# Turning the experts' gate-up product between partition groups on VectorE, in place of a trip through DRAM

## The chip, the cores and the metric

The kernel runs on one core of a Trainium2 chip. A core has TensorE (PE, matrix products; PEld is its weight load), VectorE (DVE), ScalarE (ACT), GpSimd (POOL) and SyncE (SP), each with an instruction stream of its own, and 16 DMA engines that move data between DRAM and the on-chip memories (SBUF, 128 partitions, and PSUM, where products land). Engines wait for one another through semaphores. The metric is the device time of one execution in microseconds. Three runs before the change took 3898.57, 3900.75 and 3912.13 us; the median is 3900.75.

## The reference

The reference is a decoder layer in float32 on x of shape (32, 128, 512): differential self-attention, cross-attention against a context of the same shape, and a feed-forward part with experts. The last one is what matters here, on 4096 tokens of 512 features:

```python
scores = jax.nn.sigmoid(x @ gate_w)            # 32 experts; masked by groups
_, selected_experts = jax.lax.top_k(masked_scores, K)      # K = 6
xs = x_exp[sort_idx]                           # tokens sorted by expert
g = jax.lax.ragged_dot(xs, w_gate, group_sizes)            # 512 -> 352
u = jax.lax.ragged_dot(xs, w_up, group_sizes)
d = jax.lax.ragged_dot(jax.nn.silu(g) * u, w_down, group_sizes)   # 352 -> 512
expert_out = jnp.sum(out * weights[..., None], axis=1)
shared = jax.nn.silu(x @ sw_gate) * (x @ sw_up) @ sw_down
return (expert_out + shared).reshape(B, S, H)
```

So each token goes through six experts, each expert is a gate product, an up product, their combination and a down product, and the six results are added with weights.

## The kernel before

The stages follow one another: self-attention, cross-attention with the routing, three of eight groups of the shared feed-forward part, the experts, and the other five shared groups. In the trace the experts take from about 2024 to 3617 us.

**Tiles.** Routing puts each expert's tokens into tiles of 128 slots, each tile with tokens of one expert only; 208 tiles are run. `SETS = 4` sets of weight tiles (`wg`, `wu`, `wd`) stand in SBUF, and tile i uses set i % 4. The tiles are so ordered that tiles i and i+4 mostly belong to one expert. A weight DMA has a condition (`cond=new`): it moves data only where the expert of the set changes.

**The steps of a tile i.**
- `tokens(i)` (L1422): four indirect DMAs issued by POOL gather the 128 tokens' rows from DRAM into `e_xr` (three buffers). Each row of 512 features is gathered in four runs of 128 (`Q = 4`), so that partition 32 q + k gets run q of four tokens. 
- `turn_in(i)` (L1434): one DVE turn of all 32x32 blocks makes `e_xT`, features on partitions, tokens along the row.
- `gate_up(i)` (L1447): eight gate and up products on PE (sixteen matmul instructions in the trace, since a float32 product takes two) give a PSUM tile with tokens on partitions; ACT makes Silu of the gate half (`e_act`, L1451) and DVE multiplies by the up half into `gu_s` (called `e_gu`, L1452).
- The down product needs `e_gu` with its 352 columns on partitions. DVE turns only within 32x32 blocks, that is, within a group of 32 partitions. To bring a column range of 96 (`RUN`) to each of the four groups, ACT's queue writes `e_gu` to DRAM (`e_gu_d`, L1454), and `part_out(i)` (L1463) reads it back as `e_gr`, with run q of four tokens on each partition of group q.
- `turn_out(i)` (L1473): two DVE turns, one for the first three groups (three chunks of columns) and one for the last group (two chunks, as 352 = 3 x 96 + 64), make `e_guT` (two buffers).
- `down(i)` (L1483): three chunks of products; ACT scales by the routing weight (`e_y`, L1487); POOL scatters with addition into `sum_d` in DRAM (L1488).
- `weights_in` (L1396) and `weights_out` (L1408, L1411) issue the weight DMAs on SP's queue.

Because a partition of `e_gr` holds four tokens in turn, as `e_xr` does, the order of the tokens in a turned tile is a permutation. `arrange` (L1338) lays out the gather's table so that the reading through DRAM is contiguous: it interleaves the slot numbers.

**The order.** PE, DVE, ACT and POOL run in the order in which `run` (L1508) writes the calls; SP's work is placed by the scheduler with the constraint `issue_after`. In one step of the loop the calls are: `gate_up(i)`, `turn_in(i + 2)`, `turn_out(i - 1)`, `weights_in(i + 4)`, `down(i - 2)`, `weights_out(i + 2)`, `part_out(i)`, `tokens(i + 5)`. So PE does gate and up of tile i and then down of tile i-2. ACT does Silu(i), issues the write of e_gu, scales tile i-2, and issues the read of e_gr, all in order.

Of the kernel before, what the change touches and what calls it, by code (L numbers as in the profile page):

```python
# [10 lines left out]
F32 = mybir.dt.float32  # L11
I32 = mybir.dt.int32
AF = mybir.ActivationFunctionType
ALU = mybir.AluOpType
AX = mybir.AxisListType
PSUM = bass.MemoryType.PSUM
DRAM = bass.MemoryType.DRAM

P = 128
# [9 lines left out]
M = 352  # L29
# [6 lines left out]
class Common:  # L36


    def __init__(self, tc, const, psum):
        nc = self.nc = tc.nc  # L40
        self.tc = tc
        self.psum = psum
        self.ident = const.tile([P, P], F32, name="ident")
        make_identity(nc, self.ident)
        self.mhalf = const.tile([P, 16], F32, name="mhalf")
        nc.vector.memset(self.mhalf, -0.5)
# [53 lines left out]
class Later:  # L100
# [8 lines left out]
    def run(self, step, phase):  # L109

        while self.calls and self.calls[0][0] <= (step, phase):
            _, call, args = self.calls.pop(0)
            call(*args)


def self_attention(cm, x, x1_d, Wq, Wk, Wv, Wo, lq1, lk1, lq2, lk2, heads, heads_in, beside):
# [19 lines left out]
    with ExitStack() as ctx:  # L136
# [342 lines left out]
        for n in range(len(steps) + 5):  # L479
# [29 lines left out]
            if k % 2 == 0:  # L509
                if 3 in at:  # L510
                    with behind():
                        norms(at[3][0])
                measure(b)
                if 4 in at:
                    load_again(at[4][0])
            else:
                normalize(b)
                turn_in(b)
                load(b + G)
                if 4 in at:  # L520
                    with behind():
                        scale_out(at[4][0])
                    turn_out(at[4][0])
# [4 lines left out]
class CrossAttention:  # L528
# [224 lines left out]
    def turn_out(self, b):  # L753
        o = self.out.pop(b)
        self.out[b] = self.p2.tile([P, E], F32, name="xoT")
        self.nc.vector.transpose(self.out[b], o.rearrange("p k s c -> p (k s c)"))
# [90 lines left out]
    def advance(self, count, end=None):  # L847


        steps, behind = self.steps, self.S + self.LAG  # L850
        for _ in range(count):
            n = self.at
            if n >= (self.SMALL if end is None else end):
                return
            self.at += 1
            first, sooner, middle, after, later = self.PHASES
            run = self.todo.run
            run(n, sooner)
            if 0 <= n - behind < len(steps):
                self.exponentials(*steps[n - behind])  # L860
            run(n, middle)
            if 0 <= n < len(steps):
                self.maxima(*steps[n])
            run(n, later)
# [400 lines left out]
class Experts:  # L1265
# [14 lines left out]
    def __init__(  # L1280
        self, cm, ctx, table_ds, h3_d, sum_d, w_gate, w_up, w_down, eid, fresh, rows, n_tiles
    ):
        self.cm, self.h3_d, self.sum_d, self.eid, self.fresh = cm, h3_d, sum_d, eid, fresh
        self.w_in, self.w_out, self.n_tiles = (w_gate, w_up), w_down, n_tiles
        nc, tc = cm.nc, cm.tc

        def pool(name, bufs):
            return ctx.enter_context(
                tc.tile_pool(name=name, bufs=bufs, side="right", reuse_waits="tile")
            )  # L1290

        cp, self.p2 = pool("e_c", 1), pool("e_p2", 2)
        self.dram = ctx.enter_context(tc.tile_pool(name="e_dram", bufs=4, space=DRAM))
        T = h3_d.shape[0]
        self.T, self.cp, self.rows, self.table_ds = T, cp, rows, table_ds
        self.NT = rows.shape[1]
        self.wg = [cp.tile([P, EC, M], F32, name=f"wg{s}") for s in range(SETS)]
        self.wu = [cp.tile([P, EC, M], F32, name=f"wu{s}") for s in range(SETS)]
        self.wd = [cp.tile([P, len(M_CHUNKS), E], F32, name=f"wd{s}") for s in range(SETS)]

        self.gu_s = cp.tile([P, self.Q * self.RUN], F32, name="e_gu")

        self.row_i = cp.tile([P, 2], I32, name="e_row_i")
        self.row = cp.tile([P, 2], F32, name="e_row")
        self.last, self.expert = None, {}
        self.got, self.spread = {}, {}
        self.xr, self.xT, self.gu, self.gr, self.guT = {}, {}, {}, {}, {}

    def fetch(self):

        nc = self.cm.nc
        for j in range(self.NT):
            self.got[j] = [
                self.p2.tile([P, E], F32, name=("e_y", "e_xT")[j % 2])[:, 0 : 2 * P].rearrange(
                    "p (s o) -> p s o", o=2
                )
                for i in range(len(self.table_ds))
            ]
            for t, table_d in zip(self.got[j], self.table_ds):
                nc.gpsimd.indirect_dma_start(  # L1320
                    out=t.rearrange("p s o -> p (s o)"),
                    out_offset=None,
                    in_=table_d.rearrange("(n s) o -> n (s o)", s=P),
                    in_offset=bass.IndirectOffsetOnAxis(ap=self.rows[:, j : j + 1], axis=0),
                    bounds_check=table_d.shape[0] // P - 1,
                )
        nc.gpsimd.memset(self.gu_s, 0.0)
        nc.gpsimd.iota(self.row_i, pattern=[[0, 2]], base=self.T + 1, channel_multiplier=1)

    def arrange(self, j):  # L1330

        nc = self.cm.nc
        got = self.got[j]
        nc.vector.tensor_tensor(got[0], got[0], got[1], ALU.add)
        runs = self.spread[j] = self.p2.tile([P, self.Q, self.Q, 32], F32, name="e_xr", bufs=3)
        slots = got[0][:, :, 0].rearrange("p (b t a) -> p t a b", b=self.Q, t=self.Q)
        for t in range(self.Q):
            nc.vector.tensor_copy(  # L1338
                runs[:, t].rearrange("p q (a b) -> p q a b", b=self.Q),
                slots[:, t].unsqueeze(1).broadcast_to([P, self.Q, 32 // self.Q, self.Q]),  # L1340
            )

    def turn_tables(self):
# [95 lines left out]
    def gate_up(self, i):  # L1439
        if i >= self.end:  # L1440
            return
        nc = self.cm.nc
        pgu = self.cm.banks()
        t, s = self.xT.pop(i), i % SETS
        for half, w in enumerate((self.wg[s], self.wu[s])):
            for c in range(EC):
                nc.tensor.matmul(  # L1447
                    pgu[:, half, 0:M], t[:, c, :], w[:, c, :], start=c == 0, stop=c == EC - 1
                )
        act = self.p2.tile([P, M], F32, name="e_act", bufs=1)  # L1450
        nc.scalar.activation(act, pgu[:, 0, 0:M], AF.Silu)  # L1451
        nc.vector.tensor_tensor(self.gu_s[:, 0:M], act, pgu[:, 1, 0:M], ALU.mult)  # L1452
        self.gu[i] = self.dram.tile([self.Q, P, self.RUN], F32, name="e_gu_d")
        nc.scalar.dma_start(  # L1454
            out=self.gu[i].rearrange("q s m -> s q m"),
            in_=self.gu_s.rearrange("s (q m) -> s q m", q=self.Q),
        )

    def part_out(self, i):


        gr = self.gr[i] = self.p2.tile([P, self.Q, self.RUN], F32, name="e_gr")
        self.cm.nc.scalar.dma_start(  # L1463
            out=gr.rearrange("p t m -> p (t m)"),
            in_=self.gu.pop(i).rearrange("q (i t) m -> (q i) (t m)", t=self.Q),
        )

    def turn_out(self, i):
        g = self.gr.pop(i)
        t = self.guT[i] = self.p2.tile([P, len(M_CHUNKS), P], F32, name="e_guT")  # L1470
        top = (self.Q - 1) * 32
        for rows, n in ((slice(0, top), 3), (slice(top, P), 2)):
            self.cm.nc.vector.transpose(  # L1473
                t[rows, 0:n, :].rearrange("p c (t i) -> p c t i", t=self.Q),
                g[rows, :, 0 : 32 * n].rearrange("p t (j c) -> p c t j", c=n),
            )

    def down(self, i):
        nc = self.cm.nc
# [28 lines left out]
    def run(self):  # L1508


        first, en = self.first, mybir.EngineType
        with self.cm.tc.manual_schedule(engines={en.PE, en.DVE, en.Activation, en.Pool}):
            for i in range(first, first + 2):
                self.turn_in(i)
                self.tokens(i + 3)
            for i in range(first, self.end + 2):
                self.gate_up(i)
                self.turn_in(i + 2)
                if first < i <= self.end:
                    self.turn_out(i - 1)  # L1520
                self.weights_in(i + SETS)
                if i > first + 1:
                    self.down(i - 2)
                    self.weights_out(i - 2 + SETS)
                if i < self.end:
                    self.part_out(i)
                self.tokens(i + 5)


# [180 lines left out]
```

## Time and profile before

| | us |
|---|---|
| median of three runs | 3900.75 |
| profiled execution | 3913.15 |
| its span, first to last instruction | 3911.4 |
| PE busy in the span | 3793.0 (97%) |
| DVE, ACT, POOL busy | 2057.6, 1678.9, 2349.5 |
| experts, first gate product to the end of the last down product | 2024.05 to 3617.28 |
| DVE, POOL busy in 2024 to 3620 | 535.9, 1163.2 |

In a line of the timeline stand the start, the duration, the engine, the line, the operation, out<-in with shapes, the number of instructions merged, and in brackets the idle time of the engine before it with what ended that. In a group's line stand the count, then the busy time in us and the mean of one in ns, and then the idle time before them with its main releasers. In a line of the waits stand the waiting engine with its line, what it waited for, and the sum in us, the number and the longest. "issue" stands for a wait that ended with nothing that the profile shows.

### The profile page before, as it was taken

Reading aid. Unit: us, or ns where it says so; the run is one execution under the profiler, and the core shown is the slowest. Engines: PE = TensorE matmul, PEld = TensorE weight load, DVE = VectorE, ACT = ScalarE, POOL = GpSimd, SP = SyncE. Lnnn points to the kernel's source line nnn. Section 1 sums busy time; section 2 is a strip of 40 time slices with the busy share of each in tenths; the row PEclk is TensorE's granted clock in tenths of the full one; section 3 lists DMA queues with packets and bytes.
Section 4 is the critical chain, followed back from the end, with each engine's and each line's share of the span. In section 5 each row is a group of like instructions: output and inputs, shape, how many; then the busy total and the mean of one; then the engine's idle time right before and its main releaser. Section 6 shows DMA issues by size and latency. Waiting matters only on the chain. (4 is left out here: it accounts for less than half of the span.)

```text
span 3911.4 us, 58185 instructions
## 1 busy us (share of the span) xinstructions
PE 3793.0 (97%) x19060; PEld 2015.6 (52%) x19060; DVE 2057.6 (53%) x3202; ACT 1678.9 (43%) x4032; POOL 2349.5 (60%) x2582
## 2 busy tenths in 40 slices
PE   8999999899999999999999999999999999999999
PEld 5666666434444444444445555555555555555444
DVE  5888888777877877776133333333333333332111
ACT  6989999757766776666101111111111111111000
POOL 3545545636777777775347777777777777775000
PEclk9999999899999999999999999999999999999999
DMA  3111110121111111111167777767667676766210
GB/s 110 34 34 38 37 34 27 43 87 57 53 60 47 47 47 47 49 47 50 52 178 168 164 166 170 174 151 174 160 153 167 161 170 147 181 151 150 80 64 32
DMA packets 285987, 387.21 MB, mean 99 GB/s; under 512 B 147888, under 2 KB 179248, under 8 KB 285616
## 3 DMA queue, kind: packets, MB, share of 16 engines
q0 software_dynamic: 62912, 109.85, 15.7%
q1 hardware_dynamic: 81792, 190.98, 15.4%
q10 hardware_dynamic: 140976, 82.60, 7.5%
q8 instruction: 154, 2.52, 0.3%
q14 instruction: 153, 1.25, 0.1%
HBM read 617.52 MB, written 143.07 MB: 194 GB/s over the span
## 5 line engine op out<-in xcount | busy, mean ns | idle before, releaser
L1422 POOL DMA_INDIRECT e_xr<-h_d,e_run_of x832 | 849.2, 1021 | 282.1 <-issue 268.1
L695 DVE TENSOR_REDUCE nm<-ps 128x2 f32<-128x1024 f32 x512 | 611.2, 1216 | 112.1 <-PE ps L691 105.3
L1452 DVE TENSOR_TENSOR e_gu<-e_act,ps 128x352 f32<-128x352 f32 x208 | 108.4, 521 | 974.4 <-ACT e_act L1451 548.8
L718 ACT ACTIVATE xp<-ps 128x1024 f32<-128x1024 f32 x512 | 505.9, 1021 | 265.0 <-PE ps L691 200.9
L1483 PE MATMUL ps<-wd,e_guT 128*128 128x512 f32 (+1 forms) x1248 | 585.2, 605 | 34.6 <-ACT e_y L1487 15.7
L714 PE MATMUL ps<-xqn,xk 32*128 32x512 f32 x2048 | 527.1, 620 | 20.6 <-ACT xp L718 19.2
L1447 PE MATMUL ps<-wu,e_xT 128*128 128x352 f32 x1664 | 528.6, 461 | 7.4 <-DMA wu<-in_L_ffn_w_up_dram 5.1
L1447 PE MATMUL ps<-wg,e_xT 128*128 128x352 f32 x1664 | 527.9, 460 | 5.3 <-DMA wg<-in_L_ffn_w_gate_dram 4.5
L691 PE MATMUL ps<-xk,xq 32*128 32x512 f32 x2048 | 526.9, 630 | 0.5 <-DVE nm L695 0.4
L1451 ACT ACTIVATE e_act<-ps 128x352 f32<-128x352 f32 x208 | 96.5, 464 | 935.2 <-PE ps L1447 443.7
L1488 POOL DMA_INDIRECT sum_d<-e_y,e_into x208 | 335.8, 1615 | 178.1 <-ACT e_y L1487 91.6
L1447 PEld LDWEIGHTS ps<-wg,e_xT 128*128 128x128 f32 x1664 | 315.1, 190 | 243.2 <-issue 108.8
L1447 PEld LDWEIGHTS ps<-wu,e_xT 128*128 128x128 f32 x1664 | 316.4, 191 | 186.6 <-DMA wu<-in_L_ffn_w_up_dram 8.3
L279 ACT ACTIVATE s<-s,a_nm 128x128 f32<-128x128 f32 x1024 | 395.7, 396 | 4.9 <-DVE a_nm L265 4.5
L1483 PEld LDWEIGHTS ps<-wd,e_guT 128*128 128x128 f32 (+1 forms) x1248 | 239.8, 194 | 291.7 <-issue 226.5
L1487 ACT ACTIVATE e_y<-ps,e_weight 128x512 f32<-128x512 f32 x208 | 143.0, 687 | 431.3 <-PE ps L1483 265.0
L714 PEld LDWEIGHTS ps<-xqn,xk 32*128 32x128 f32 x2048 | 168.6, 183 | 284.3 <-ACT xp L718 123.3
L1473 DVE STREAM_TRANSPOSE e_guT<-e_gr 96x384 f32<-96x384 f32 (+1 forms) x416 | 230.5, 554 | 76.2 <-DMA e_gr<-e_gu_d 53.5
L228 POOL TENSOR_SCALAR k<-kz,a_keep,a_extra 128x256 f32<-128x256 f32 x128 | 82.6, 655 | 287.4 <-ACT kz L227 287.4
L1028 POOL DMA_INDIRECT table_d<-entry,at x192 | 202.1, 1053 | 64.7 <-issue 53.2
L729 PE MATMUL ps<-xp,v 128*32 128x512 f32 x2048 | 233.0, 595 | 7.9 <-ACT xp L718 7.6
L1434 DVE STREAM_TRANSPOSE e_xT<-e_xr 128x512 f32<-128x512 f32 x208 | 226.3, 1088 | 8.8 <-DMA e_xr<-h_d,e_run_of 8.8
(272 smaller groups left out, 5282.6 us busy)
## 6 DMA issues: line engine op xcount, KB each, us to landing
wg<-in_L_ffn_w_gate_dram SPq DMA_DIRECT2D x208, 704.0 KB
wu<-in_L_ffn_w_up_dram SPq DMA_DIRECT2D x208, 704.0 KB
wd<-in_L_ffn_w_down_dram SPq DMA_DIRECT2D x208, 576.0 KB
e_gu_d<-e_gu ACTq DMA_DIRECT2D x208, 192.0 KB
e_gr<-e_gu_d ACTq DMA_DIRECT2D x208, 192.0 KB
wd<-in_L_ffn_w_down_dram SPq DMA_DIRECT2D x208, 128.0 KB
e_xr<-h_d,e_run_of POOLq DMA_INDIRECT x832
xres<-in_x_dram SPq DMA_DIRECT2D x32, 256.0 KB
```

The lines of the kernel that those rows point to most:

```text
L279: nc.scalar.activation(s[:, j, c, side, :], s[:, j, c, side, :], AF.Exp, bias=nm[n][:, side, at : at + 1], accum_out=sm[n][:, to : to + 1],)
L691: self.nc.tensor.matmul(sc[:, i, :], q[rows, ts(c, P)], k[rows, :], start=True, stop=True)
L695: self.nc.vector.tensor_reduce(at[:, self.ROW[side], 2 * pair : 2 * pair + 2], sc, AX.X, ALU.max, negate=True)
L714: self.nc.tensor.matmul(sc[:, i, :], k[rows, ts(c, P)], q[rows, :], start=True, stop=True)
L718: self.nc.scalar.activation(e, sc, AF.Exp)
L729: self.nc.tensor.matmul(po[b, side][ts(j, 32), :], self.v2[b % 2][:, c, 2 * j + side, :], es[j // 2][:, j % 2, :], start=c == 0, stop=c == ...
L1422: self.cm.nc.gpsimd.indirect_dma_start(out=xr[:, t, :], out_offset=None, in_=self.h3_d.rearrange("t (q f) -> (t q) f", q=self.Q), in_offse ...
L1434: self.cm.nc.vector.transpose(xT.rearrange("p c (t i) -> p c t i", t=self.Q), self.xr.pop(i).rearrange("p t (j c) -> p c t j", c=EC),)
L1447: nc.tensor.matmul(pgu[:, half, 0:M], t[:, c, :], w[:, c, :], start=c == 0, stop=c == EC - 1)
L1473: self.cm.nc.vector.transpose(t[rows, 0:n, :].rearrange("p c (t i) -> p c t i", t=self.Q), g[rows, :, 0 : 32 * n].rearrange("p t (j c) -> ...
L1483: nc.tensor.matmul(py, t[:n, c, :], self.wd[s][:n, c, :], start=c == 0, stop=c == len(M_CHUNKS) - 1)
L1488: nc.gpsimd.indirect_dma_start(out=self.sum_d[:, :], out_offset=bass.IndirectOffsetOnAxis(ap=self.into[:, i : i + 1], axis=0), in_=y[:, :] ...
```

## The change

The trip through DRAM goes: `part_out`, the DRAM pool, `e_gr` and the zeroing of `e_gu` are removed, and ACT issues no DMA in the stage any more. `e_gu` has 352 columns in place of 384. `turn_out(i)` is now sixteen DVE turns: for each partition group q of the result and each group s of 32 tokens, one turn reads `e_gu` on the partitions of group s, in the column range of q, and writes the turned blocks to the partitions of group q. For q = 0, 1, 2 one turn covers three 32x32 blocks (96 columns), for q = 3 two (64). It is called in the step of its own tile, right after `gate_up(i)` and ahead of `turn_in(i + 2)`. The tokens keep their order: `arrange` copies the slot numbers in runs of 32 as they stand. The number of gathers, products, scatters and weight DMAs is what it was.

```diff
-        self.gu_s = cp.tile([P, self.Q * self.RUN], F32, name="e_gu")
+        self.gu_s = cp.tile([P, M], F32, name="e_gu")
...
-        nc.gpsimd.memset(self.gu_s, 0.0)
...
-        slots = got[0][:, :, 0].rearrange("p (b t a) -> p t a b", b=self.Q, t=self.Q)
         for t in range(self.Q):
             nc.vector.tensor_copy(
-                runs[:, t].rearrange("p q (a b) -> p q a b", b=self.Q),
-                slots[:, t].unsqueeze(1).broadcast_to([P, self.Q, 32 // self.Q, self.Q]),
+                runs[:, t], got[0][:, ts(t, 32), 0].unsqueeze(1).broadcast_to([P, self.Q, 32])
             )
...
-        nc.vector.tensor_tensor(self.gu_s[:, 0:M], act, pgu[:, 1, 0:M], ALU.mult)
-        self.gu[i] = self.dram.tile([self.Q, P, self.RUN], F32, name="e_gu_d")
-        nc.scalar.dma_start(
-            out=self.gu[i].rearrange("q s m -> s q m"),
-            in_=self.gu_s.rearrange("s (q m) -> s q m", q=self.Q),
-        )
-
-    def part_out(self, i):
-        gr = self.gr[i] = self.p2.tile([P, self.Q, self.RUN], F32, name="e_gr")
-        self.cm.nc.scalar.dma_start(
-            out=gr.rearrange("p t m -> p (t m)"),
-            in_=self.gu.pop(i).rearrange("q (i t) m -> (q i) (t m)", t=self.Q),
-        )
+        nc.vector.tensor_tensor(self.gu_s, act, pgu[:, 1, 0:M], ALU.mult)
 
     def turn_out(self, i):
-        g = self.gr.pop(i)
+        if not self.first <= i < self.end:
+            return
         t = self.guT[i] = self.p2.tile([P, len(M_CHUNKS), P], F32, name="e_guT")
-        top = (self.Q - 1) * 32
-        for rows, n in ((slice(0, top), 3), (slice(top, P), 2)):
-            self.cm.nc.vector.transpose(
-                t[rows, 0:n, :].rearrange("p c (t i) -> p c t i", t=self.Q),
-                g[rows, :, 0 : 32 * n].rearrange("p t (j c) -> p c t j", c=n),
-            )
+        for q in range(self.Q):
+            n = min(self.RUN, M - q * self.RUN) // 32
+            for s in range(self.Q):
+                self.cm.nc.vector.transpose(
+                    t[ts(q, 32), 0:n, ts(s, 32)],
+                    self.gu_s[ts(s, 32), ds(q * self.RUN, 32 * n)].rearrange(
+                        "p (j c) -> p c j", c=n
+                    ),
+                )
...
                 self.gate_up(i)
+                self.turn_out(i)
                 self.turn_in(i + 2)
-                if first < i <= self.end:
-                    self.turn_out(i - 1)
                 self.weights_in(i + SETS)
                 if i > first + 1:
                     self.down(i - 2)
                     self.weights_out(i - 2 + SETS)
-                if i < self.end:
-                    self.part_out(i)
                 self.tokens(i + 5)
```

## The prediction

> **What bounds the kernel now.** The change touches the expert stage alone, so I first read that stretch by itself (the view of busy time by stretches), then the waits of PE and of the queues, then the timeline around one wait.
>
> ```profile
> 2024.00:3620.00 1596.00, 1547.26 (x4581) 871.99 (x4580) 535.94 (x831) 238.96 (x416) 1163.24 (x1019) 0.99 0.69 162
> ```
>
> The columns are the length, then PE, PEld, DVE, ACT and POOL busy, the granted clock, the DMA share and GB/s. PE is busy 97% of 1596 us; DVE has only 536 us of work, 2.6 us per tile. So PE is the bound, and what matters is the little that it loses. In the timeline of PE:
>
> ```profile
> 2045.67 2.74 PE L1483 MATMUL ps<-wd,e_guT 128*128 128x512 f32 x6
> 2048.25 2.53 PE L1447 MATMUL ps<-wg,e_xT 128*128 128x352 f32 x8
> 2050.61 2.53 PE L1447 MATMUL ps<-wu,e_xT 128*128 128x352 f32 x8
> 2052.98 2.74 PE L1483 MATMUL ps<-wd,e_guT 128*128 128x512 f32 x6
> ...
> 3570.03 0.46 ACT L1451 ACTIVATE e_act<-ps 128x352 f32<-128x352 f32 x1 [9.51 <-PE ps L1447]
> ...
> 3573.17 5.46 PE L1483 MATMUL ps<-wd,e_guT 128*128 128x512 f32 x6 [4.09 <-DVE e_guT L1473]
> ```
>
> An undisturbed tile takes 2052.98 - 2045.67 = 7.31 us from start to start (2.37 + 2.36 gate and up, 2.58 down). The last two lines are a disturbance: a Silu that could have run at about 3561.8 (its products ended at 3561.61) ran at 3570.03, so e_guT came late, PE idled 4.09 us, and the next six matmuls took 5.46 us in place of 2.74: PE ran on at half speed for a while.
>
> What the stage loses: the first gate product starts at 2024.05, the last at 3600.73, 207 tiles later. Two fill tiles take 9.57 us (to 2033.62), 205 clean ones would take 205 x 7.31 = 1498.6; together 1508.2. It took 1576.7, so **68 us are lost**. The waits of PE in the stage name the idle part of it:
>
> ```profile
> PE ps L1483 <- ACT e_y L1487: 15.7, 7, 3.1
> PE ps L1483 <- issue: 6.6, 6, 2.0
> PE ps L1483 <- DVE e_guT L1473: 6.3, 2, 4.1
> PE ps L1483 <- DMA wd<-in_L_ffn_w_down_dram: 5.9, 3, 2.2
> PE ps L1447 <- DMA wu<-in_L_ffn_w_up_dram: 5.1, 3, 2.8
> PE ps L1447 <- DMA wg<-in_L_ffn_w_gate_dram: 4.5, 4, 2.5
> ...
> SPq L1411 <- DMA wd<-in_L_ffn_w_down_dram: 218.7, 59, 9.6
> SPq L1411 <- DMA e_gr<-e_gu_d: 76.0, 23, 6.2
> ```
>
> With 3.1 us more on L1447 they sum to 47.2, of which 2.0 lie in the tail: 45 us idle inside the stage; the other 23 of the 68 are the half-speed matmuls after a wait. Of the idle, 15.5 us name weights, 29.7 name ACT, e_guT or nothing, all of which stand behind the trip of e_gu through DRAM, since ACT issues both its DMAs in order with Silu (L1451) and the scaling (L1487). The two SP lines show that the weight queue itself stood 295 us at L1411, in part for that trip.
>
> **The change part by part.** *Removed: two DMAs per tile on ACT's queue* (L1454, L1463). Their queue carries this share of the 16 DMA engines in 2050 to 3600 us:
>
> ```profile
> q10 hardware_dynamic: 136037, 79.70, 18.3%
> ```
>
> ACT is left with two activations, 0.46 + 0.69 = 1.15 us per 7.31, which wait for PE, for DVE's reading of e_act and for the scatter that frees e_y. So the 29.7 us idle and their half-speed share go. Weights: the DMA share falls from 0.69 to about 0.51, and SP no longer stands for e_gr. Their 15.5 us cost 15.5 x 68/45 = 23 us now; I keep 6 (bounds 0 and 23, nearer 0 because the largest competitor for the same moments is gone and each weight has more than three tiles of lead: issued after the product of tile i, used by tile i+4).
>
> *Added: sixteen turns on DVE in place of two.* The rows, from the groups kept apart by shape:
>
> ```profile
> L1434 DVE STREAM_TRANSPOSE e_xT<-e_xr 128x512 f32<-128x512 f32 x206 | 224.1, 1088 | 0.0
> L1473 DVE STREAM_TRANSPOSE e_guT<-e_gr 96x384 f32<-96x384 f32 x208 | 138.7, 667 | 73.3 <-DMA e_gr<-e_gu_d 53.5 <-issue 16.0 <-SPq L1644 3.7
> L1473 DVE STREAM_TRANSPOSE e_guT<-e_gr 32x256 f32<-32x256 f32 x208 | 91.8, 441 | 2.8
> L393 DVE STREAM_TRANSPOSE anT<-an 128x512 f32<-128x512 f32 x32 | 22.8, 711 | 1.0
> ```
>
> 711 for 512 elements read plainly and 441 for 256 read every second one lie on 171 + 1.055 N. Read every third, 384 take 667, or 171 + 1.29 N. The new turns keep these strides: twelve of 96 elements at 171 + 124 = 295 ns, four of 64 at 238. Two turns in a row do not overlap now: the timeline has
>
> ```profile
> 2030.03 1.10 DVE L1434 STREAM_TRANSPOSE e_xT<-e_xr 128x512 f32<-128x512 f32 x1
> ...
> 2034.82 1.09 DVE L1434 STREAM_TRANSPOSE e_xT<-e_xr 128x512 f32<-128x512 f32 x1
> 2035.84 1.11 DVE L1473 STREAM_TRANSPOSE e_guT<-e_gr 96x384 f32<-96x384 f32 x2
> ```
>
> and 0.667 + 0.441 = 1.11, so I add about 14 ns between turns: 12 x 0.309 + 4 x 0.252 = **4.7 us per tile**, against 1.1 before. (The e_xT turn ahead does overlap, 2034.82 + 1.09 > 2035.84, by 0.07; were all turns so, it would be 16 x 0.07 less than 4.5, that is 3.4.) The Trainium skill, "VectorE: DVE Perf Modes", section "Two Vector instructions with no wait between them", speaks against the change here: an instruction that starts in another group of 32 partitions than the one ahead is held until all earlier ones are done, and here every turn does. By it the sum is 4.7, without it 3.4; the row shows one such pair, and both sums end hidden.
>
> DVE's tile is then 0.52 + 4.7 + 1.09 and some 0.05 of handing over = 6.4 us of 7.31: beside PE, if nothing makes it wait. Bounds for a turn: below, 0.18 us, the 128x32 elementwise row (L1014, 179 ns); above, 0.441, the 32x256 turn. I take the fit, as both rows it joins are this instruction. If the extra of the third-element stride were fixed per instruction (667 - 576 = 91 ns), the sum would be 12 x 0.377 + 4 x 0.252 = 5.5, still under the 5.7 that DVE has.
>
> *Moved: the turn stands ahead of turn_in(i+2), and has a wait.* e_guT has two buffers, and turn_out(i) is now written before down(i-2) has read the older one, so its first turn waits for PE. With T the end of gate_up(i): down(i-2) ends at T+2.6, turns run T+2.8 to T+7.5, turn_in(i+2) to T+8.6, and gate_up(i+2) starts at T+9.9: 1.3 us to spare. Queued behind on DVE is the product of tile i+1 (its Silu is done at T+8.0; it runs at T+8.6 to 9.1), whose turns wait for T+10.1 anyway. On POOL the gathers of tile i+5 (L1422) wait for turn_in(i+2): released at T+8.6, where the scatter ahead freed them at about T+5.5. POOL's own round is 4 x (1.02 + 0.30) + 1.62 + 0.30 = 7.2 us, under 7.31; the gathered rows are used 20 us later, so it is hidden, with 0.1 us of cover per tile. The scatter of tile i-1 (L1488) is queued behind these gathers, from T+13.9 where it was ready at T+10.9; its e_y is rewritten at T+24.8, 9 us after its issue ends. SP is moved past nothing.
>
> *Start.* In the fill there is no down, so the turns of tile 0 delay turn_in(2): product done 2030.11, turns to 2034.8, e_xT at 2035.9, where its product started at 2033.62: 2.3 us, and some 1.5 of half speed (2.7 followed the wait of 4.09; in proportion). *End.* The last down waits for its turns: T+7.7 against 3612.77 - 3605.47 = T+7.3: 0.4 us. *Rest:* POOL's memset of e_gu goes (0.4 us), arrange's eight copies keep their 128 elements, the gathers keep 128 rows each: nothing, as PE runs the shared stage meanwhile.
>
> Sum against the profiled execution's 3913.15: - 68 + 6 + 3.8 + 0.4 = **3855**. The median of the three runs, 3900.75, lies 12.4 below that execution. If the difference is fewer stalls, the new time stays at 3855; if it lies in other stages, 3843. I take 3852.
>
> **The rivals.**
> - *Weights still wait.* For: 15.5 us of PE's idle names them, and L1411 stands 218.7 us for wd itself. Against: their landing slows in the same moments as the trip that goes. Price: 23 in place of 6, 3872; up to 3890 if stalls now put down to nothing (6.6 + 3.1, times 1.5) are theirs as well.
> - *DVE becomes the bound (slower).* It decides from 5.7 us of turns per tile, 0.354 us from turn to turn, 18% over my fit. For: turns between partition groups and of 32 partitions by 96 elements occur nowhere in the trace, and the start-up cost may be more. Price: at 0.40, (16 x 0.046) x 207 = 152, 4007; at the upper bound 0.455 with its gap, 335, 4190.
> - *POOL becomes the bound.* Cover is 0.1 us per tile. If DVE's longer work slowed each gather by 0.05 us, the round is 7.4, and 0.09 x 207 = 19: 3874. Against: gathers beside a turn take 1.01 us as the others do. The Trainium skill, "SBUF — State Buffer", in its box on DVE blocking DMA, has descriptor writing locked out while VectorE runs a two-port mode; the turns' 1.055 ns per element shows no doubled rate, so that would add nothing.
> - *No change:* the stalls are the weight bursts themselves and merely change their name: 3890 to 3910.
>
> **How the numbers follow.** Forecast 0.70 (3836 to 3862), weights 0.12, POOL 0.05, no change 0.04, DVE 0.09. The range 3836 to 3890 holds the first three and leaves out the last two. About 0.5% is what a measurement of this kernel can tell from no change, 19.5 us: faster is below 3881. That is the forecast, POOL, and most of the weights' case: 0.85; same 0.05; slower 0.10.
>
> **What would show it.** Right: 7.31 us per tile nearly throughout, the stage some 60 us shorter; turns of about 0.295 and 0.238 us, one after the other; L1451's idle naming PE alone; no wait over 10 us in total on PE for ACT; DVE some 1300 us in the stage; one PE wait for e_xT near the start. Wrong: a period of 7.4 or more in clean stretches, PE waiting for e_xT tile after tile (DVE), gathers naming nothing but themselves at 7.31 or more (POOL), or the same weight waits as before.

## The result, and the profile after

The changed kernel took 3932.7 us (median of four runs, 3927.4 to 3935.1) against 3903.2 for the kernel before (four runs): **1.0065 of it, 95% interval 1.0046 to 1.0085**. It is 0.65% slower, where the forecast was 3852 and a range of 3836 to 3890. The profiled execution took 3933.0 us with a span of 3931.3.

The same views as before, of the kernel after. Busy time by stretches, for the experts (length; PE, PEld, DVE, ACT, POOL busy; granted clock; DMA share; GB/s):

```profile
2024.00:3640.00 1616.00, 1556.91 (x4582) 878.66 (x4581) 1264.37 (x3743) 236.20 (x416) 1164.43 (x1020) 0.98 0.50 109
```

DVE went from 536 to 1264 us and the DMA share from 0.69 to 0.50, as forecast. The stage, from the first gate product to the end of the last down product, went from 1593.2 to 1612.3 us (2023.94 to 3636.23). By the prediction's own way of counting, first to last gate product less 1508.2 of clean tiles, it now loses 87 us (1595.7 - 1508.2) where it lost 68. The groups of the same stretch, kept apart by shape:

```profile
L1418 POOL DMA_INDIRECT e_xr<-h_d,e_run_of x812 | 828.8, 1021 | 346.9 <-issue 222.9 <-DVE e_xT L1430 116.6 <-DMA sum_d<-e_y,e_into 5.2
L1457 DVE STREAM_TRANSPOSE e_guT<-e_gu 32x96 f32<-32x96 f32 x2496 | 745.1, 299 | 206.2 <-PE ps L1469 115.2 <-remote 22.5 <-issue 22.3
...
L1443 PE MATMUL ps<-wg,e_xT 128*128 128x352 f32 x1664 | 550.3, 475 | 55.9 <-issue 42.9 <-ACT e_y L1473 10.0 <-ACT e_act L1447 2.5
...
L1457 DVE STREAM_TRANSPOSE e_guT<-e_gu 32x64 f32<-32x64 f32 x832 | 198.8, 239 | 11.1
```

The new turns (L1457) cost 299 and 239 ns, the forecast 295 and 238. The gate product (L1443, the one that reads e_xT) has 55.9 us of idle time before it; no weight and no DMA is named. Its mean of 475 ns, against 460 of the up product, is the half-speed running after such a wait. The timeline around one wait shows the path:

```profile
2799.67 1.64 PE L1443 MATMUL ps<-wu,e_xT 128*128 128x352 f32 x5
...
2805.27 0.46 ACT L1447 ACTIVATE e_act<-ps 128x352 f32<-128x352 f32 x1 [7.28 <-PE ps L1469]
...
2808.18 4.73 DVE L1457 STREAM_TRANSPOSE e_guT<-e_gu 32x96 f32<-32x96 f32 x16 [1.90 <-remote]
...
2812.95 1.08 DVE L1430 STREAM_TRANSPOSE e_xT<-e_xr 128x512 f32<-128x512 f32 x1
...
2814.13 2.10 PE L1443 MATMUL ps<-wg,e_xT 128*128 128x352 f32 x3 [2.92 <-issue]
```

The up product ends at 2801.31, by its record. Its Silu on ACT starts at 2805.27: **4 us later, and ACT did nothing else in between** (it idled 7.28 us, and what ended that is PE; "remote" stands for a release whose source the profile does not tell). The sixteen turns, the turn of e_xT and the next gate product follow late, and PE stands for 2.92 us. I call the time from the end of the last up product to the start of its Silu the *lateness* of PE's report. Worked out from the trace over the tiles 3 to 202 (counted from 0), it is 1.21 us on average after the change, and over 2 us in 63 of these tiles. It is not new: in the kernel before it is 1.18 us on average and up to 8.3. The path is the one of this wait throughout: before the gate products PE idles 32 times, 55.7 us in all, and each time the product starts within 0.3 us of the end of its turn of e_xT.

### The profile page after: what moved, and what is told of

Read it like the earlier page. It is cut to its first block, busy times and chain, and to the rows that moved or that the text cites. A ratio compares the mean times of both kernels' runs of the same rounds, so it can differ in the third digit from the quotient of the medians.

```text
span 3931.3 us, 60267 instructions
## 1 busy us (share of the span) xinstructions
PE 3802.2 (97%) x19060; PEld 2021.7 (51%) x19060; DVE 2785.2 (71%) x6114; ACT 1675.4 (43%) x4032; POOL 2348.9 (60%) x2581
## 5 line engine op out<-in xcount | busy, mean ns | idle before, releaser
L1457 DVE STREAM_TRANSPOSE e_guT<-e_gu 32x96 f32<-32x96 f32 (+1 forms) x3328 | 943.9, 284 | 217.3 <-PE ps L1469 115.2
L718 ACT ACTIVATE xp<-ps 128x1024 f32<-128x1024 f32 x512 | 505.7, 1021 | 265.2 <-PE ps L691 197.1
L1443 PE MATMUL ps<-wg,e_xT 128*128 128x352 f32 x1664 | 550.3, 475 | 55.9 <-issue 42.9
L1469 PE MATMUL ps<-wd,e_guT 128*128 128x512 f32 (+1 forms) x1248 | 571.3, 593 | 2.3 <-issue 2.3
L1443 PE MATMUL ps<-wu,e_xT 128*128 128x352 f32 x1664 | 528.0, 460 | 0.0
L1443 PEld LDWEIGHTS ps<-wg,e_xT 128*128 128x128 f32 x1664 | 321.2, 195 | 308.8 <-issue 158.4
L1443 PEld LDWEIGHTS ps<-wu,e_xT 128*128 128x128 f32 x1664 | 318.4, 191 | 178.7 <-issue 4.5
L279 ACT ACTIVATION_READ_ACCUMULATOR s<-s,a_nm 128x1 f32 x1024 | 199.2, 195 | 0.0
```

Source lines behind the costliest of these rows:

```text
L279: nc.scalar.activation(s[:, j, c, side, :], s[:, j, c, side, :], AF.Exp, bias=nm[n][:, side, at : at + 1], accum_out=sm[n][:, to : to + 1],)
L718: self.nc.scalar.activation(e, sc, AF.Exp)
L1443: nc.tensor.matmul(pgu[:, half, 0:M], t[:, c, :], w[:, c, :], start=c == 0, stop=c == EC - 1)
L1457: self.cm.nc.vector.transpose(t[ts(q, 32), 0:n, ts(s, 32)], self.gu_s[ts(s, 32), ds(q * self.RUN, 32 * n)].rearrange("p (j c) -> p c j", c=n),
L1469: nc.tensor.matmul(py, t[:n, c, :], self.wd[s][:n, c, :], start=c == 0, stop=c == len(M_CHUNKS) - 1)
```

## The experiments

Each set of kernels ran on one chip, with the kernel before beside it. The sets fell on different chips, and the chips differ: the kernel before took 3866 us on chip B, 3854 on C, 3901 on D, 3910 on E, 3854 on F (A is the chip of the result, 3903). Ratios are therefore to the kernel before on the same chip. "Stage" runs from the first gate product to the end of the last down product, "idle" is PE's idle time in it, "late" the mean lateness, all from the profiled execution. In the expectations, the *cover* of a tile is the time by which it stands ready before PE needs it when nothing is late.

| chip | kernel | us | ratio, 95% interval | stage | idle | late |
|---|---|---|---|---|---|---|
| A | before | 3903.2 | 1 | 1593.2 | 47.3 | 1.18 |
| A | after | 3932.7 | 1.0065 (1.0046 to 1.0085) | 1612.3 | 58.2 | 1.21 |
| B | e1 turn of e_xT first | 3855.9 | 0.9971 (0.9960 to 0.9982) | 1540.6 | 11.3 | 2.74 |
| B | e2 three e_guT | 3862.6 | 0.9993 (0.9983 to 1.0002) | 1543.5 | 15.7 | 0.95 |
| B | e3 turn of e_xT halfway | 3876.8 | 1.0023 (1.0014 to 1.0033) | 1556.3 | 23.3 | 1.50 |
| B | e4 both | 3853.1 | 0.9976 (0.9965 to 0.9987) | 1530.8 | 6.4 | 2.71 |
| C | f1 after | 3848.2 | 0.9986 (0.9977 to 0.9996) | 1527.8 | 4.6 | 0.04 |
| C | f2 after, no gathers | 3848.5 | 0.9986 (0.9976 to 0.9996) | 1527.7 | 4.6 | 0.04 |
| C | f3 before, no gathers | 3850.1 | 0.9985 (0.9975 to 0.9995) | 1527.5 | 3.4 | 0.12 |
| C | f4 after, no weights | 3844.8 | one run | 1526.2 | 4.6 | 0.04 |
| D | g1 after, five Silus | 3974.4 | 1.0182 (1.0159 to 1.0205) | 1662.3 | 92.3 | 0.97 |
| D | g2 before, five Silus | 3939.9 | 1.0096 (1.0067 to 1.0124) | 1617.4 | 70.7 | 1.66 |
| D | g3 e1, five Silus | 3927.4 | 1.0071 (1.0047 to 1.0096) | 1605.9 | 58.5 | 2.58 |
| D | g4 after, no gathers | 3846.6 | one run | 1527.8 | 4.6 | 0.04 |
| E | i1 after | 3930.4 | 1.0074 (1.0051 to 1.0098) | 1597.1 | 50.7 | 1.25 |
| E | i2 before, no gathers | 3847.4 | 0.9850 (0.9829 to 0.9871) | 1528.3 | 4.4 | 0.12 |
| E | i3 after, short gathers | 3933.7 | 1.0061 (1.0038 to 1.0085) | 1614.2 | 60.8 | 1.19 |
| E | i4 both | 3902.7 | 0.9983 (0.9971 to 0.9995) | 1581.1 | 39.1 | 2.87 |
| F | k1 both, later scatter | 3843.6 | 0.9971 (0.9960 to 0.9981) | 1522.1 | 0.8 | 0.04 |
| F | k2 after, two gathers | 3847.6 | 0.9986 (0.9976 to 0.9995) | 1527.8 | 4.6 | 0.04 |

i1's profiled execution is the fastest of its six (3915.6 to 3937.7), so its stage stands low beside i3's.

### Where the turn of e_xT stands, and how many buffers e_guT has (chip B)

e1, e2 and e3; e4 is e1 and e2 together:

```diff
# e1
                 self.gate_up(i)
-                self.turn_out(i)
                 self.turn_in(i + 2)
+                self.turn_out(i)
# e2
-        t = self.guT[i] = self.p2.tile([P, len(M_CHUNKS), P], F32, name="e_guT")
+        t = self.guT[i] = self.p2.tile([P, len(M_CHUNKS), P], F32, name="e_guT", bufs=3)
# e3
-                self.turn_out(i)
+                self.turn_out(i, (0, 1))
                 self.turn_in(i + 2)
+                self.turn_out(i, (2, 3))
```

> The changed kernel with turn_in(i+2) ahead of turn_out(i) on DVE; nothing else. Theory A (thin cover): what PE ends becomes known to ACT and DVE late, by 1.2 us on average and up to 5 to 8 (as much in the kernel before as in the changed one), and the changed kernel leaves e_xT only 1.2 us of cover, so lateness above that is lost. Here e_xT has some 7.5 us and e_guT some 7: the time falls to 3845 to 3860, PE idles under 10 us in the stage, and the Silu still starts late by about 1.2 us on average. Theory B (load): the sixteen turns make DVE too full, wherever they stand: 3915 to 3935. Theory C (the lateness comes from PE's sequencer standing in a wait for e_xT, 5.5 us per tile in the changed kernel): 3845 to 3860 as well, but the Silu is no longer late (under 0.3 us on average).

> The changed kernel with three buffers for e_guT, so that the turns wait for no down product; turn_in stays behind them. A: the cover of e_xT grows from 1.2 to about 2.8 us, and the lateness that counts is that of the Silu; the sums of lateness above 2.8 us in the two traces are 31 and 58 us in place of 60 above 1.2 in the changed kernel: 3875 to 3915. B: 3915 to 3935, no better. C: PE's sequencer still stands some 3 us per tile, so the Silu is late by less than 1.2 us but not by nothing.

> The changed kernel with turn_in(i+2) between the eighth and the ninth turn. A: cover of e_xT about 3.5 us; lateness of the down product above it sums to 12 to 29 us: 3860 to 3890, between e1 and the changed kernel. B: 3915 to 3935.

> turn_in first and three buffers for e_guT. A: no wait is left that e1 has not already covered: 3845 to 3860, the same as e1 within 0.3%. If the wait for the down product itself costs something beside e_xT's cover, it is below e1 by that much.

Measured: in the table. The waits of PE in the stage, in e1:

```profile
PE ps L1469 <- issue: 5.4, 5, 2.3
PE ps L1443 <- issue: 4.8, 10, 1.0
...
PE ps L1443 <- ACT e_y L1473: 1.0, 1, 1.0
```

Theory B falls: e1 has the same sixteen turns on DVE as e3 and differs from it by their place alone; it is 21 us faster than e3 and faster than the kernel before. (The changed kernel itself was not run on this chip.) Theory C falls too: it wanted the Silu on time in e1, but there it is later than anywhere else on this chip (2.74 us). Theory A's mechanism stands, that the place of the turn decides whether a late report reaches PE: each longer wait of PE for e_xT in e1 (ten over 0.3 us) follows a Silu 8.1 to 9.4 us late, more than the cover of some 7.5. Its numbers for e2 and its "1.2 us late" for e1 missed: the chip is a milder one, and with the turn of e_xT first the reports are later (2.74 and 2.71 us, against 0.95 and 1.50 in e2 and e3).

### What makes the reports late (chips C, D, E)

The reports are on time in the stages before and after the experts (in the kernel before, 858 of the 861 waits of ACT, DVE and POOL there that PE ended were over within 0.14 us of the product's end), and among what only the experts' stage has are POOL's gathers and the conditional weight DMAs. f2, f3, g4 and i2 leave the gathers out; `kept` holds the first three tiles' rows. f4 returns from `weights_in` and `weights_out` ahead of their DMAs from the fifth tile on. i3 cuts the rows, k2 keeps two gathers of four:

```diff
# f2, g4 (and f3, i2 on the kernel before)
-        xr = self.xr[i] = self.p2.tile([P, self.Q, P], F32, name="e_xr", bufs=3)
-        for t in range(self.Q):
+        if i >= self.first + 3:
+            self.xr[i] = self.kept[i % 3]
+        ...
+        for t in range(self.Q if i < self.first + 3 else 0):
# i3, instead of the last line; n is 128 for the first three tiles, then 8
+        for t in range(self.Q):
-                out=xr[:, t, :],
+                out=xr[:, t, 0:n],
-                in_=self.h3_d.rearrange("t (q f) -> (t q) f", q=self.Q),
+                in_=self.h3_d.rearrange("t (q f) -> (t q) f", f=n),
```

> The changed kernel unaltered, on one chip with the three runs that follow. Where it was first measured it took 3932.7 us against 3903.2 of the kernel before; the kernel before took 3866.2 where the four kernels with the moved turn ran, so the chips differ. All theories: slower than the kernel before by 10 to 35 us, tensor engine idle in the experts' stage 40 to 65 us, the Silu 1 to 1.5 us late on average behind the end of the up product.

> The changed kernel with the token gathers left out from the fourth tile on (the first three tiles' tokens are used again; weights, turns, products and scatters stay; that part of the computation is missing). Theory P (the tensor engine's reports of finished work are held up while GpSimd works on its indirect gathers, four of 1.02 us and one scatter of 1.61 us in each 7.31 us): Silu less than 0.2 us late, tensor engine idle in the stage under 10 us, 3835 to 3860. Theory W (they are held up by transfers, the weights' above all): Silu still 0.8 us late or more, time within 15 us of the changed kernel's. Theory N (neither; the tensor engine's own queue): as W.

> The kernel before, trip through DRAM kept, with the token gathers left out from the fourth tile on in the same way (that part of the computation is missing). Theory P: Silu less than 0.2 us late and tensor engine idle in the stage under 10 us although the gate-up product still goes through DRAM and the scalar engine still issues both transfers in order; 3835 to 3855. The prediction's reading (the trip and the scalar engine's order make the product late): idle as in the kernel before, some 30 us or more, and a time within 10 us of it. Theories W and N: the same, with the Silu 0.8 us late or more.

> The changed kernel with the experts' weights loaded for the first tiles only and used again (that part of the computation is missing; gathers, turns and scatters stay). Theory W: Silu less than 0.2 us late, idle under 10 us, 3835 to 3860. Theories P and N: Silu 0.8 us late or more and a time within 15 us of the changed kernel's.

Chip C told nothing of these theories and something else instead: f2 and f3 came out as P had it and f4 as W had it, since nothing is late there to begin with. With all its gathers, f1 has no late report at all: the largest lateness is 0.04 us. f1's expectation, slower by 10 to 35 us, missed; it is faster than the kernel before by 0.14%. Its timeline is the undisturbed tile:

```profile
2801.12 2.53 PE L1443 MATMUL ps<-wu,e_xT 128*128 128x352 f32 x8
...
2803.49 2.74 PE L1469 MATMUL ps<-wd,e_guT 128*128 128x512 f32 x6
...
2803.68 0.46 ACT L1447 ACTIVATE e_act<-ps 128x352 f32<-128x352 f32 x1 [4.05 <-PE ps L1443]
...
2806.26 4.74 DVE L1457 STREAM_TRANSPOSE e_guT<-e_gu 32x96 f32<-32x96 f32 x16 [1.02 <-PE ps L1469]
...
2811.03 1.10 DVE L1430 STREAM_TRANSPOSE e_xT<-e_xr 128x512 f32<-128x512 f32 x1
...
2813.38 2.53 PE L1443 MATMUL ps<-wg,e_xT 128*128 128x352 f32 x8
```

The up product ends at 2803.65 and the Silu starts at 2803.68. The turns wait for the down product of the tile two before (to 2806.23, the two buffers), e_xT is done at 2812.13, and its product starts at 2813.38 with no wait: 1.25 us to spare.

> The changed kernel without the token gathers from the fourth tile on (that part of the computation is missing), once more, for a chip on which the reports are late. There, theory P (GpSimd's gathers hold them up): first Silu less than 0.2 us behind the up product although it is more than 0.5 us behind in the three runs before; theory N: as late as in those. On a chip where reports come at once: 3840 to 3855, as the last time, and nothing is told apart.

> The changed kernel unaltered, beside the next three. Where the tensor engine's reports come late (the kernel before takes 3860 or more): 3905 to 3940, 20 to 40 us slower than the kernel before. Where they come at once (the kernel before at 3853): 3848.

> The kernel before without the token gathers from the fourth tile on (that part of the computation is missing), trip through DRAM kept. Where reports are late, theory P (the gathers hold them up, and they alone cost the kernel before its idle time): 3845 to 3855, Silu less than 0.2 us late. The prediction's reading (the trip itself, with the scalar engine's order): 25 us or less under the kernel before. Where reports come at once: 3845 to 3855 for both, nothing told apart.

> The changed kernel with each gathered row cut from 128 to 8 numbers from the fourth tile on: as many gathers, indices and rows, a sixteenth of the bytes (the rest of the rows is left from the first tiles; that part of the computation is missing). Where reports are late: if it is GpSimd's work on the gathers that holds them up, the Silu is as late as in the changed kernel beside it and the time within 20 us of it; if it is the bytes moved, Silu less than 0.2 us late and 3843 to 3855.

On chips D and E the reports are late, and there the theories part. g4 is the changed kernel without gathers: 3846.6 us where the kernel before takes 3901, and the lateness is 0.04. i2 is the **kernel before, trip through DRAM and all**, without gathers: 3847.4 us beside 3909.7, lateness 0.12. Its waits of PE in the stage:

```profile
PE ps L1490 <- issue: 1.8, 1, 1.8
...
PE ps L1454 <- DMA wg<-in_L_ffn_w_gate_dram: 1.2, 1, 1.2
PE ps L1454 <- ACT e_y L1494: 0.8, 1, 0.8
PE ps L1454 <- DMA wu<-in_L_ffn_w_up_dram: 0.6, 1, 0.6
```

Of 47.3 us idle in the kernel before on chip A, 4.4 are left; the weights' 15.5 are 1.8, with the trip's transfers still beside them. (The 0.12 us holds ACT's own work: it still issues the trip's transfers.) i3 tells the instructions from the bytes. Its gathers move a sixteenth, and its groups and waits read:

```profile
L1426 POOL DMA_INDIRECT e_xr<-h_d,e_run_of x812 | 831.3, 1024 | 343.9 <-issue 220.5 <-DVE e_xT L1438 115.2 <-DMA sum_d<-e_y,e_into 5.5
```

```profile
PE ps L1451 <- issue: 47.1, 24, 4.4
...
PE ps L1451 <- ACT e_y L1481: 10.7, 7, 2.0
```

A short gather takes POOL as long (1024 ns), the lateness is 1.19, and the time is that of i1 within 4 us. So it is the gathers that hold up PE's reports, and not the bytes that they move. N falls, and W falls as a cause by itself, since the weights are all there in g4 and i2.

Of theory P the gathers are shown, but not that it is POOL's own work on them: i3 has as many gathers, rows and landings, and each landing updates a semaphore 16 times (820 gathers fewer in f2 than in f1 are 13110 such updates fewer in the trace). A second rival is the recording itself. Where reports are late, the trace also lacks records of semaphore updates: 37977 stand in f1, 22783 in i1 with the same kernel, and of 596 updates that PE's matmuls had to make between 2024 and 3560 us in the kernel after 455 are recorded, where g4, i2 and all runs on C and F lack at most one. Every run on record has a granted clock from the profiler, so none shows whether the reports are as late when nothing is recorded.

### A late product, made on purpose (chip D)

```diff
-        nc.scalar.activation(act, pgu[:, 0, 0:M], AF.Silu)
+        for _ in range(5):
+            nc.scalar.activation(act, pgu[:, 0, 0:M], AF.Silu)
```

> The changed kernel with the Silu of each tile done five times over into the same tile, so that the product's result is some 1.9 us later (4 x 0.46) wherever the tensor engine's reports come at once. Theory K (what counts is each kernel's cover against a late product: 1.24 us here, from the end of the turn of e_xT to its product on the chip without late reports): the product of tile i+2 starts (1.9 - 1.24) us late every two tiles, 0.3 us per tile, some 60 to 70 us: 3900 to 3930 on a chip with reports 0.04 us late, more on one where they are late by themselves. Theory L (a steady 1.9 us is taken up somewhere, only the rare long delays cost): within 15 us of the changed kernel's 3848.

> The kernel before with the same four extra Silus. Theory K: its cover is 4.0 us (from the turn of e_guT to the down product), so 1.9 us cost nothing: 3848 to 3865 on a chip with reports that come at once, and against its own time on the same chip at most 15 us more. Theory L: the same. If the trip through DRAM itself is at its limit, 30 us more or above.

> The changed kernel with the turn of e_xT ahead of the sixteen turns, and the same four extra Silus. Theory K: the product of the next but one tile no longer waits for the sixteen turns, and the 1.9 us cost nothing: 3843 to 3862 where reports come at once. If it is the vector engine's load that makes a late product dear, it loses as much as the changed kernel with four extra Silus, 3900 or more.

The chip has late reports of its own, so 1.9 us came on top of them, and g1 is at 3974, above the 3900 to 3930 of a prompt chip, as said. g3, with the turn of e_xT first, is 47 us faster than g1 with the same work on every engine: order alone, though it stays 26 us over the kernel before. But theory K had g2 at no more than 15 us over the kernel before, and it is 39 us over, which is also what was expected of a trip at its limit.

The traces tell the two apart. In the kernel before on chip A, 13 of the 18 idle times of PE before a down product (25.7 of 34.5 us) lie one tile ahead of a Silu that is over 4 us late, whose product stands ahead of this tile's turn on DVE, and 12 of them are that Silu's lateness less 4.0 to 4.2 us: 4.1 us idle for a Silu 8.3 late, 3.1 for 7.2, 2.2 for 6.4. In g2, with a Silu over 2.1 us late, it is 49 of 55 (61.9 of 68.3 us), mostly the lateness less 2.2. So a cover of about 4 us hides a late report of up to 4 us, but not 1.9 more on top of it. Whether 1.9 us alone cost nothing was not run on a chip with prompt reports.

### A version for both kinds of chip (chips E, F)

i4 is e4 again. k1 is e4 with the scatter of a tile issued one tile later on POOL and three buffers of e_y:

```diff
                     self.down(i - 2)
                     self.weights_out(i - 2 + SETS)
+                if i > first + 2:
+                    self.scatter(i - 3)
```

> The changed kernel with the turn of e_xT first and three buffers of e_guT, to see whether it beats both kernels on one chip with them. Theory K (cover against late reports decides): the covers are 7.7 us for e_xT and 6 us for e_guT against 4.0 of the kernel before, so where reports are late 3850 to 3885, at least 20 us under the kernel before; where they come at once 3843 to 3850.

> The version with both covers, and each tile's scatter issued one tile later on GpSimd, with three buffers of e_y. Theory M (what is left there is GpSimd, 98% taken by five instructions a tile, waiting for e_y): its wait for e_y goes from 76 us to under 15, and the time to 3850 to 3875 on a chip where the kernel before takes 3900 or more, 3845 to 3855 where it takes 3860 or less. Theory R (reports back up as long as GpSimd has no pause, so a wait taken away comes back as a later report): mean lateness of the Silu above the 2.9 us of the version with both covers, a time within 15 us of its 0.998 of the kernel before.

> The changed kernel with two of the four gathers left out from the fourth tile on (that part of the computation is missing), so that GpSimd has 2.6 us without an instruction in each tile. Theory R: the reports get through in the pause; Silu less than 0.4 us late on average and 3843 to 3860 on any chip. If each gather holds up a report by itself: lateness about half the changed kernel's 1.2 us, and, on a chip where the kernel before takes 3900, 3870 to 3900.

On chip E, i4 takes 3902.7: 27.7 us less than the changed kernel and 0.17% less than the kernel before, but not the 3850 to 3885 expected. The reports got later, 2.87 us on average and up to 13, as in e1 and e4 on chip B. The waits of POOL and PE in i4's stage:

```profile
POOL sum_d L1474 <- ACT e_y L1473: 80.1, 41, 4.2
...
PE ps L1443 <- ACT e_act L1447: 20.8, 11, 2.7
...
POOL sum_d L1474 <- ACT e_act L1447: 13.5, 8, 4.0
...
PE ps L1443 <- issue: 10.9, 14, 1.8
```

POOL, whose round of five instructions takes 7.2 us of 7.31, waits for a late e_y. That is not what PE stands for, however: before each of its 19 idle times over 0.3 us ahead of a gate product, the gathers of that tile had ended 12 to 17 us before its turn, and the Silu two tiles earlier was 8.2 to 13.0 us late, more than the 7.7 us of cover. The covers work as expected; the reports are later. k1 was to remove POOL's wait, and k2 to give POOL a pause, but chip F has no late reports. There k1 is the fastest version, 0.9971 of the kernel before, with 0.8 us of idle left; whether it helps where reports are late (theory M or R) stays open, and so does what half the gathers do.

## Why the prediction was wrong, step by step

**What the stage loses, and to what: the step that failed.** It read "29.7 name ACT, e_guT or nothing, all of which stand behind the trip of e_gu through DRAM, since ACT issues both its DMAs in order", and "So the 29.7 us idle and their half-speed share go". The 68 us were there, but i2 keeps the trip and PE idles 4.4 us: what made the tiles late were PE's reports, held up where the gathers run, and the idle times of the kernel before follow the lateness of single Silus (25.7 of 34.5 us before the down products). Where reports come at once, the whole change brings 5 us (3853.5 to 3848.2 on chip C), and without gathers the kernels with and without the trip lie 1.6 us apart there (f3, f2). The sign of it was in the lines shown ahead of the forecast: the Silu at 3570.03, whose product ended at 3561.8 by its record, had its wait ended by *PE*, not by a DMA. The trace's records of PE's semaphore confirm it: four updates, which products that ended from 3561.8 to 3569.1 had to make, came in a burst at 3569.95, 3570.03, 3570.12 and 3570.21. ACT was not late; it was told late. I took a wait on PE as a mark of what stood behind ACT.

**Weights: within the bounds, the cause open.** 6 us were kept of 23. No weight is named after the change on chip A, where reports are as late as before; but i2 has only 1.8 us with the trip kept. So the waits for weights go without the trip or without the late reports, and which of the two the relief came from is not told apart. A release of a weight set is also a report of PE; that this is how the weights came late was only argued.

**The turns: right.** 299 and 239 ns, sixteen in 4.73 us against 4.7, DVE hidden. 12 x 299 + 4 x 239 is 4.54, so 13 ns lie between turns. The Trainium skill, "VectorE: DVE Perf Modes", section "Two Vector instructions with no wait between them", has an instruction that starts in another group of 32 partitions held until all earlier ones are done; the 13 ns agree with it, and the 3.4 us of overlapped turns did not come. (In the rival with DVE as the bound, 0.354 us from turn to turn is 20% over the fit's 0.295, not 18.)

**The moved turn: the times right, the verdict wrong.** "1.3 us to spare" is 1.25 in f1. But that was weighed against none of the lateness that the trace of before shows. From the traces without late reports, the kernel before has 4.0 us to spare at its tightest place, from the turn of e_guT to the down product (f3, median). The change takes the 1.1 us turns and the trip off the path to the down product, whose spare time is then 7.1 us, and puts 4.73 us of turns onto the path to the next but one gate product, where 7.6 us became 1.25. The sizes agree: in the kernel after, what each down product's report is late beyond 1.2 us adds to 59.6 us over the tiles, and PE idles 58.2; on chip E, 53.8 and 50.7. On chip A the idle time also stands where this path ends, before the gate products. The order alone takes 21 us (e1 against e3) and 47 us (g3 against g1) away, and with a third buffer besides it leaves no loss on chip E (i4). So the order is what turned a gain of 5 us into a loss of 20 to 30; e1 itself was not run on A or E.

**POOL.** Forecast: hidden, with 0.1 us of cover per tile. On chip C its gathers wait 19.3 us for e_xT, and nothing comes of it. On A the wait is 116.6 us, behind the same late turn. The gathers, those beside turns among them, take 1021 ns on average as before, so the two-port rule weighed there added nothing, as said.

**Start: right.** 2.3 us of waiting and 1.5 of half speed were forecast:

```profile
2034.79 1.08 DVE L1430 STREAM_TRANSPOSE e_xT<-e_xr 128x512 f32<-128x512 f32 x1
...
2035.97 4.19 PE L1443 MATMUL ps<-wg,e_xT 128*128 128x352 f32 x8 [2.30 <-issue]
```

4.19 against 2.53 of a full-speed product is 1.66.

**The sum.** On a chip with prompt reports it comes out, 3848 against 3852, but by luck: the kernel before is at 3854 there too. None of the rivals named a late report; the slower one, DVE as the bound, was not what happened, since the period between disturbances stayed 7.31 us.

## What to carry to other kernels

Before an idle time is put down to a step in the middle of a chain, compare the end of the producing instruction with the start of its consumer and read which engine ended the consumer's wait: a consumer that idles and is released by an engine long done was told late, and shortening what stands after it helps only by the spare time that it leaves. Weigh the spare time of a moved instruction against the lateness that the trace already shows, not against zero; and put the short work that the bound engine waits for next ahead of the long work that it needs later. Compare two kernels on one chip: here the chip alone moved the kernel before from 3854 to 3910, and turned the verdict on the change around.

## What the runs showed of the hardware

- PE's reports reached the other engines up to 13 us late in the stage in which POOL issues indirect gathers (four of 1.02 us and a scatter of 1.61 us in each 7.31 us), on chips A, B, D and E (13.0 in i4, 8.3 in the kernel before); on C and F, with POOL instructions of the same length, 0.04 us in every tile where ACT does not issue the trip. (A may be the same chip as D or E.) Without the gathers they were prompt on D and E. Cutting the rows to a sixteenth changed nothing. Why some chips do this is open, as are the path on which a report is held and the part that recording the semaphore updates has in it.
- The lateness builds up over several tiles, in one stretch of e1 from 0.7 to 7.8 us in three, and is gone in one or two. In the same stretch three reports came 0.09 us apart at 2272.05 to 2272.23, while POOL had a pause from 2271.1 to 2273.0. With the turn of e_xT first it grows: on chip B from 0.95 us (e2) to 2.7 (e1, e4), on D from 0.97 (g1) to 2.58 (g3), on E from 1.25 (i1) to 2.87 (i4). That it is a pause of POOL that lets the reports through was not shown, as k2 fell on a chip without late reports.
- The half-speed running after a wait does not go in proportion to it. In the kernel after, i1 and i3, from the third gate product on, all 63 waits of 0.1 to 2.0 us before a gate product were followed by a product of 2.60 us, and all 24 of 2.7 us or more by one of 3.7 to 5.0; of the 13 between, 9 were followed by a slow one.
